# Turning the normed tiles of a second pass through DRAM and VectorE instead of TensorE

## Chip, core and metric

The kernel runs on one core of one Trainium2 chip. The time is device microseconds of the whole launch; before the change three runs took 3366.73, 3371.97 and 3379.04 us, median 3371.97. Everything is 32-bit float.

## What is computed

Two layers in a row on 8 images of 32 x 32 positions and 512 channels. The first is group norm, multi-head attention and a residual. The second samples 256 places of the image by learned offsets (a depthwise convolution, gelu, a small projection, tanh, bilinear gather), attends from all 1,024 positions to these, projects, adds the input, and ends with a layer norm and a gelu layer. The part that the change touches is the end of the second layer:

```python
z = msa + x                      # msa = att @ mo_w + mo_b
z_ln = layernorm(z, ln_g, ln_b)
out = gelu(z_ln @ mlp_w + mlp_b) + z
```

The kernel folds `ln_g` into the weights (`wm = ln_g * mlp_w`) and `ln_b` into the bias row `bm_row`, so that only `(z - mean) * rstd` has to be turned and multiplied.

## The kernel before

The first pass (layer one) runs to about 2100 us and is not touched. The second pass works by half images: `hi` from 0 to 15, each half with 512 query positions, and by head pairs `hp` from 0 to 3. One head pair of one half image is a unit, n = 4 hi + hp, 64 in all.

The order of work is written out by hand. `at(place, step)` puts a step on a list, and `run_due` sorts the list by place and calls the steps, each of which issues its instructions on all engines. Each engine then keeps this program order, since `InOrder` (L43) tells the scheduler to. So a place such as n + 0.03 sets only what stands before what on each engine; it is no time. A unit's steps in `unit_steps` (L1188) are: the scores at n; the first head's turned weights written to DRAM (`moved`, L134) at n + 0.02; the sums turned and written (`share`) at n + 0.039; the second head's turned weights at n + 0.04; both read back (`taken`, L147) and the sums spread (`spread`) up to n + 0.0411; the next unit's query projection at n + 0.042; the product with the values at n + 1.1, that is in the next unit; and its scaling to `attH` at n + 1.2.

The attention weights are thus turned already in the way that the change uses elsewhere: VectorE's `transpose` works within blocks of 32 x 32, and writing to DRAM and reading back in another order moves whole blocks between partitions.

`back_steps` (L1107) ends a half image: four tiles of 128 positions, one per unit, at n = 4 (hi + 1) + 1 + t. A tile's steps are `fetch` (the input rows `xr`, by SP's queue), `add` (on GpSimd), `joined` (output projection `wo`, sum `z` and its statistics), `norm` (`zn`, on VectorE), `turned` (four TensorE transposes of 128 x 128 into PSUM and two ScalarE copies to `zT`), `mlp` (the product with `wm`), `biased` (`res`, on VectorE), and by pairs of tiles `gelu` and `end` (the sum with `z` and the store, on GpSimd). `turned` stands at n + 0.6, behind the product of the unit before; `mlp` of a tile stands in the next unit, behind that unit's `joined`. On TensorE a unit therefore reads: scores, `wo` product, `wm` product of the tile before, queries, product with values, four transposes.

Beside this run, up to about unit 41, the last eight chunks of the depthwise convolution (`conv_steps`, L1217), in two lanes: lane 0 multiplies and adds on VectorE, five taps to a unit and three in units with n mod 8 of 3, 4 or 6; lane 1 multiplies on ScalarE into `parts` and adds on GpSimd, seven taps to a unit. And `point_steps` (L1242) prepares the sampled places of the next image b: `corners` on VectorE, `gather` (four indirect DMAs) and `sample` (four VectorE operations over 512 words) for each half of the places. With last = 8 b - 4, the samples stand at last + 0.0415 and last + 2.0415, ahead of that unit's scaling, and keys and values follow in the unit with n mod 8 = 7 and after.

`load_small` (L867) and `load_late` (L1258) load vectors and weights before unit 0. The SP queue issues DMAs in program order, and an instruction that waits there holds up those behind it.

Of the kernel before, what the change touches and what calls it, by code (L numbers as in the profile page):

```python
# [9 lines left out]
F32 = mybir.dt.float32  # L10
I32 = mybir.dt.int32
AF = mybir.ActivationFunctionType
ALU = mybir.AluOpType
# [4 lines left out]
P = 128  # L18
# [3 lines left out]
C = 512  # L22
NC = C // P
# [11 lines left out]
SQ = 32  # L35
NSQ = P // SQ
# [211 lines left out]
def attention_then_deformable_attention(  # L248
# [30 lines left out]
    nc = tc.nc  # L279
# [4 lines left out]
    dram = ctx.enter_context(tc.tile_pool(name="dram", bufs=1, space=DRAM))  # L284
# [18 lines left out]
    def load_w(pool, w, name):  # L303
        t = pool.tile([P, NC, w.shape[1]], F32, tag=name, name=name)
        nc.sync.dma_start(t, by_chunk(w))
        return t
# [100 lines left out]
    with ExitStack() as l0:  # L407
# [3 lines left out]
        nc = InOrder(tc)  # L411
# [383 lines left out]
        for b in range(B):  # L795
            first = b * per
            for hp in range(1, NHP):
                places = first_places if b == 0 else pair_places
# [19 lines left out]
            for hp in range(NHP):  # L818
                for qt in range(NT):
                    n = first + hp * NT + qt  # L820
                    if n % per == 0 and b > 0:
# [6 lines left out]
                    t = qkv[b, hp]  # L828
# [5 lines left out]
                        q=t["q", qt // NQT][:, ts(qt % NQT, P)],  # L834
# [8 lines left out]
    with ExitStack() as l1:  # L843
        nc = tc.nc
# [22 lines left out]
        def load_small():  # L867
            with nc.allow_non_contiguous_dma(reason="small vectors onto partitions"):
                for t, v in (
                    (bvk, mk_b), (bv_c, bv), (bvv, mv_b), (bqq, mq_b), (bq_c, bq), (lng, ln_g),  # L870
                    (lnb, ln_b),
                ):
                    nc.sync.dma_start(t, v.rearrange("(c p) -> p c", p=P))

        def load_conv():
            with nc.allow_non_contiguous_dma(reason="small vectors onto partitions"):
# [227 lines left out]
        def tmp(name, bufs):  # L1104
            return work.tile([P, C], F32, tag=name, name=name, bufs=bufs)

        def back_steps(hi, start, step, tail=False):  # L1107

            b, half = divmod(hi, 2)
            xs = mid[b].rearrange("(t p e) c -> e t p c", e=2, p=P)[half]  # L1110
            outs = out_tok[b].rearrange("(t p e) c -> e t p c", e=2, p=P)[half]
            xr, z, zn, zT, res = {}, {}, {}, {}, {}
            n_units = 2 * B * NHP

            def fetch(t):
                xr[t] = tmp("xr", 4)
                nc.sync.dma_start(xr[t], xs[t])

            def add(t):
                nc.gpsimd.tensor_tensor(xr[t], xr[t], bo_row, ALU.add)  # L1120

            def joined(t):
                ps = project(lambda c: attH[hi][:, c, ts(t, P)], lambda c: wo[:, c, :])
                z[t] = tmp("z", 4)
                nc.vector.tensor_tensor(z[t], ps, xr[t], ALU.add)
                stats = work.tile([P, 6], F32, tag="stats", name="stats")
                mv = xr["mv", t] = work.tile([P, 3], F32, tag="mv", name="mv")
                nc.vector.bn_stats(stats, z[t])
                nc.vector.bn_aggr(mv[:, 0:2], stats)
                rstd(mv[:, 2:3], mv[:, 1:2], 1e-5)  # L1130

            def norm(t):
                zn[t], mv = tmp("zn", 2), xr["mv", t]
                nc.vector.tensor_scalar(
                    zn[t], z[t], mv[:, 0:1], mv[:, 2:3], ALU.subtract, ALU.mult
                )

            def turned(t):
                ps = mm_tile()
                for c in range(NC):  # L1140
                    nc.tensor.transpose(ps[:, ts(c, P)], zn[t][:, ts(c, P)], ident)
                zT[t] = tmp("zT", 2)
                for half in range(2):
                    nc.scalar.copy(zT[t][:, ts(half, C // 2)], ps[:, ts(half, C // 2)])

            def mlp(t):
                res["ps", t] = project(lambda c: zT[t][:, ts(c, P)], lambda c: wm[:, c, :])

            def biased(t):
                res[t] = tmp("res", 3)  # L1150
                nc.vector.tensor_tensor(res[t], res["ps", t], bm_row, ALU.add)

            def gelu(t):
                nc.scalar.activation(res[t], res[t], AF.Gelu)

            def end(t):
                (nc.vector if tail else nc.gpsimd).tensor_tensor(res[t], res[t], z[t], ALU.add)
                (nc.sync if tail else nc.gpsimd).dma_start(outs[t], res[t])

            for t in range(NC):  # L1160
                over, eve = (start + step * t >= n_units - i and not tail for i in range(2))
                n, pair = start + step * t, start + step * (t - t % 2)

                ends = (n + 0.6, n + 1.03, n + 1.0392)
                if eve:
                    ends = (n + 0.61, n + 0.72, n + 0.73) if over else (n + 1.06, n + 1.62, n + 1.625)
                places = (pair - 1.6, pair - 0.5), (n + 0.012, n + 0.03), ends
                if tail:
                    turn = n + 0.15 + 0.005 * (t > 0)
                    places = (n - 0.7, n - 0.6), (n, n + 0.01), (turn, n + 0.25, n + 0.26)  # L1170
                steps = (fetch, add), (joined, norm), (turned, mlp, biased)
                for place, what in zip(sum(places, ()), sum(steps, ())):
                    at(place, lambda t=t, what=what: what(t))


                ends = [t - 1, t] if t % 2 and not tail else [t] if tail else []

                for what, after in (
                    (gelu, 0.27 if tail else 0.735 if over else 1.72),
                    (end, 0.28 if tail else 0.74 if over else 2.24),  # L1180
                ):
                    for i in ends:
                        at(n + after, lambda i=i, what=what: what(i))
# [33 lines left out]
        def conv_steps():  # L1217
            for lane, chunks in enumerate(((0, 3, 6), (1, 2, 4, 5, 7))):
                free = 0.5 + lane
                for k in chunks:  # L1220
                    b, cb = EARLY + k // NC, k % NC
                    first = next(n for n in range(60) if n + 0.49 > free)
                    fills = [first + 0.49, first + 0.55]
                    at(fills[0] - 1.8, lambda b=b, cb=cb: conv_fetch(b, cb))
                    for par, place in enumerate(fills):
                        at(place, lambda b=b, cb=cb, par=par: fill(b, cb, par))
                        at(place + 0.02, lambda lane=lane, par=par: fill_end(lane, par))
                    unit = int(fills[1]) + 1
                    i = 0
                    while i < KS * KS:  # L1230
                        points = unit % (2 * NHP) in (NHP - 1, NHP, NHP + 2)
                        count = 7 if lane else 3 if points else 5
                        for j in range(count):
                            if i == KS * KS:
                                break
                            place = 0.25 + 0.01 * j if not lane else 0.045 + 0.001 * j if j < 4 else 0.65 + 0.01 * j
                            at(unit + place, lambda b=b, cb=cb, i=i, lane=lane: tap(b, cb, i, lane))
                            free = unit + place
                            i += 1
                        unit += 1  # L1240

        def point_steps(b):  # L1242
            last = 2 * NHP * b - NHP
            at(last - 3.5, lambda: conv_load(b))
            at(last - 2.035, lambda: conv_gelu(b))
            at(last - 1.465, lambda: offsets(b))
            at(last - 1.36, lambda: offsets_turned(b))
            at(last - 0.959, lambda: targets(b))
            for h, (p0, p1) in enumerate(((-0.28, 0.0415), (1.72, 2.0415))):
                at(last + p0, lambda h=h: gather(b, h))  # L1250
                at(last + p1, lambda h=h: sample(b, h))
            first = 2 * NHP * b
            for hp, place in enumerate((-0.82, -0.815, 0.185, 1.18)):
                at(first + place, lambda hp=hp: key_step(b, hp))
            for t, place in enumerate((-0.81, 0.18)):
                at(first + place, lambda t=t: value_step(b, t))

        def load_late():  # L1258
            nonlocal bq_row, wo, wm, bo_row, bm_row
            bq_row = load_row(wp, bq, "bq_row")  # L1260
            wo = load_w(late2, mo_w, "wo")
            wm = load_w(late2, mlp_w, "wm")
            bo_row = load_row(late, mo_b, "bo_row")
            bm_row = load_row(late2, mlp_b, "bm_row")
            load_conv()
# [66 lines left out]
```

## Time and profile before

| | |
|---|---|
| median of three runs | 3371.97 us |
| profiled execution, whole | 3374.83 us |
| its span, first to last instruction | 3373.1 us |
| TensorE busy | 3282.7 us, 97% |
| VectorE busy | 2490.4 us, 74% |
| ScalarE busy | 1809.0 us, 54% |
| GpSimd busy | 1548.1 us, 46% |
| mean granted TensorE clock | 0.991 |

Groups of instructions that the change touches, all in the second pass, as the view by groups gives them:

| engine, operation | count | busy us | mean ns of one |
|---|---|---|---|
| PE, transposes of zn | 256 | 41.8 | 286 |
| ScalarE, copies to zT | 128 | 41.1 | 373 |
| VectorE, zn from z | 64 | 39.4 | 615 |
| VectorE, sq from e (128 x 1,024 words) | 640 | 766.1 | 1228 |
| VectorE, rsT from rs (128 x 32 words) | 128 | 27.1 | 212 |
| VectorE, taps of lane 0 | 144 | 109.4 | 760 |
| VectorE, samples (first of four, and the others) | 16 and 48 | 8.6 and 58.0 | 540 and 1209 |
| PE, wm product | 1024 | 230.7 | 592 |

Matmuls overlap in TensorE's pipeline, so the mean of one is longer than the busy time divided by the count. All instructions carry line 54, since a helper issues them; they are told apart by the tiles they write and read, written out<-in. From issue to landing a DMA took, in the median, 2.7 us (sq_d), 4.5 us (et from sq_d), 2.4 us (rs_d), 5.3 us (inv) and 6.0 us (xr).

### The profile page before, as it was taken

How to read it: one execution, taken by the hardware profiler on the slowest of the kernel's cores; microseconds unless marked ns; L12 is line 12 of the kernel's file. 1: busy time of each engine (PE TensorE's matmuls, PEld its weight loads, DVE VectorE, ACT ScalarE, POOL GpSimd, SP SyncE). 2: the span in 40 equal slices, each digit the busy share in tenths (PEclk: the TensorE clock that was granted, in tenths of full speed). 3: DMA queues.
4: the chain of work that ended last, by engine and by line, in shares of the span. 5: the costliest groups of instructions: out<-in, count | busy, mean ns of one | idle time of the engine just before them, and what ended most of it. 6: DMA issues, size and time to landing. Idle time of an engine off the chain costs nothing. (4 is left out here: it accounts for less than half of the span.)

```text
span 3373.1 us, 59630 instructions
## 1 busy us (share of the span) xinstructions
PE 3282.7 (97%) x21736; PEld 1339.8 (40%) x21736; DVE 2490.4 (74%) x3373; ACT 1809.0 (54%) x3927; POOL 1548.1 (46%) x1903
## 2 busy tenths in 40 slices
PE   7999999999999999999999998889999999999998
PEld 3344444444444344344344443433333333333333
DVE  5777788888888898888888886238667686665654
ACT  3443355576566566567567562135556555654442
POOL 1001226646746755764765663305555454642222
PEclk9999999999999999999999999999999999999999
DMA  5666766776766776766777766546666665665653
GB/s 150 179 179 164 209 181 186 223 182 183 214 188 181 210 201 181 210 197 183 204 196 184 203 193 180 170 139 220 192 206 198 191 200 187 214 218 191 224 181 127
DMA packets 446645, 642.56 MB, mean 190 GB/s; under 512 B 77105, under 2 KB 240945, under 8 KB 444305
## 3 DMA queue, kind: packets, MB, share of 16 engines
q1 hardware_dynamic: 415712, 536.67, 55.0%
q0 software_dynamic: 29488, 100.00, 9.7%
q8 instruction: 172, 2.82, 0.4%
q10 hardware_dynamic: 1152, 2.10, 0.2%
q14 instruction: 121, 0.98, 0.1%
HBM read 246.38 MB, written 123.73 MB: 110 GB/s over the span
## 5 line engine op out<-in xcount | busy, mean ns | idle before, releaser
L54 ACT ACTIVATE e<-sc,nmax 128x1024 f32<-128x1024 f32 (+1 forms) x1024 | 802.0, 796 | 494.5 <-DVE nmax L54 493.1
L54 DVE TENSOR_REDUCE nmax<-sc 128x1 f32<-128x1024 f32 (+1 forms) x640 | 751.3, 1214 | 337.5 <-PE sc L54 336.8
L54 POOL TENSOR_TENSOR oa<-part_x,oa 128x256 f32<-128x256 f32 x852 | 639.6, 751 | 554.0 <-ACT part_x L54 507.6
L54 DVE STREAM_TRANSPOSE sq<-e 128x1024 f32<-128x1024 f32 x640 | 766.1, 1228 | 155.8 <-ACT e L54 134.6
L54 ACT ACTIVATE part_x<-pad_x,dww_x 128x256 f32<-128x256 f32 x852 | 440.9, 545 | 250.3 <-POOL oa L54 249.4
L54 PE MATMUL sc<-k,q 64*64 64x512 f32 x4096 | 516.6, 602 | 13.5 <-ACT e L54 10.3
L54 PE MATMUL av<-et,v 128*64 128x256 f32 x4096 | 502.1, 388 | 15.1 <-DMA et<-sq 14.2
L54 PE MATMUL mm<-xT,wqkv 128*64 128x512 f32 x2048 | 463.5, 595 | 3.2 <-issue 3.2
L54 PEld LDWEIGHTS av<-et,v 128*64 128x64 f32 x4096 | 275.5, 137 | 332.6 <-issue 169.8
L54 POOL TENSOR_TENSOR chunk<-parts,chunk 128x256 f32<-128x256 f32 x240 | 188.8, 787 | 268.5 <-ACT parts L54 254.5
L54 POOL TENSOR_TENSOR mv<-mv,minus_half 128x1 f32<-128x1 f32 x128 | 76.3, 596 | 510.4 <-DVE mv L54 509.8
L54 PEld LDWEIGHTS sc<-k,q 64*64 64x64 f32 x4096 | 139.3, 132 | 321.8 <-issue 205.0
L54 PEld LDWEIGHTS mm<-xT,wqkv 128*64 128x64 f32 x2048 | 148.6, 138 | 255.0 <-issue 239.6
L54 DVE SCALAR_TENSOR_TENSOR od<-pad_x,dww_x,od 128x256 f32<-128x256 f32 x276 | 232.0, 841 | 5.5
L54 PE MATMUL mm<-wo,attH 128*64 128x512 f32 x1024 | 233.7, 598 | 0.0
L54 PE MATMUL mm<-wqkv,xT 128*64 128x256 f32 x2048 | 232.1, 379 | 0.0
L54 PE MATMUL mm<-wm,zT 128*64 128x512 f32 x1024 | 230.7, 592 | 1.0 <-ACT zT L54 1.0
L54 PE MATMUL mm<-w,attT 128*64 128x512 f32 x1024 | 229.8, 592 | 1.8 <-DVE attT L54 1.8
L54 PE MATMUL mm<-hat_h,wqq 128*64 128x512 f32 x1024 | 230.8, 593 | 0.0
L54 ACT ACTIVATION_READ_ACCUMULATOR e<-sc,nmax 128x1 f32 x1024 | 209.3, 204 | 0.0
L54 ACT ACTIVATE parts<-pad,dww 128x256 f32<-128x256 f32 x240 | 126.4, 551 | 126.8 <-POOL chunk L54 125.9
L54 PEld LDWEIGHTS mm<-wqkv,xT 128*64 128x64 f32 x2048 | 147.9, 137 | 77.8 <-issue 6.4
(164 smaller groups left out, 3361.8 us busy)
## 6 DMA issues: line engine op xcount, KB each, us to landing
et<-sq SPq DMA_DIRECT2D x2048, 128.0 KB, 2.8
sq_d<-sq SPq DMA_DIRECT2D x128, 512.0 KB, 2.7
et<-sq_d SPq DMA_DIRECT2D x128, 512.0 KB, 4.5
inv<-rs_d SPq DMA_DIRECT2D x256, 128.0 KB, 5.3
hat_h<-hat_d SPq DMA_DIRECT2D x16, 1024.0 KB, 8.4
xr<-mid SPq DMA_DIRECT2D x64, 256.0 KB, 6.0
x<-in_x_dram POOLq DMA_DIRECT2D x60, 256.0 KB, 4.4
out_dram<-res POOLq DMA_DIRECT2D x60, 256.0 KB, 3.6
```

The costliest lines, as they stand in the source:

```text
L54: return self.tc.keep_in_program_order(op(*args, **kwargs))
```

## The change

For 58 of the 64 tiles `turned` is replaced by three steps. `away` (n + 0.0301, right behind `norm`) writes `zn` to a DRAM tile in four DMAs, one for each 32 partitions, in runs of 128 words. `back` (n + 0.0395, behind the sums' write and ahead of the second head's turned weights) reads it in one DMA, 512 words in a row for each partition, into another buffer of the `zn` tag. `blocks` (n + 0.21, behind the scaling) turns it on VectorE in 32 x 32 blocks into `zT`. The last two tiles of the order before the end and the four of the last half image keep `turned`; there `norm` writes its columns in another order (`by_matmul`).

A turned tile now has its channels in another order over the partitions: partition 32 r + i of chunk c holds channel 128 r + 32 c + i. So `wm`, `lng` and `lnb` are loaded in that order, each in four DMAs of 32 partitions.

Other places move too. `fetch` and `add` of a pair of tiles come one unit earlier (from pair - 1.6 and pair - 0.5 to pair - 2.6 and pair - 1.45). `end` goes from 2.24 to 2.0125, ahead of the lane 1 taps of its unit. Both `sample` steps go from 0.0415 to 0.22 of their unit, behind `attH`'s scaling and behind `blocks`. Lane 0 has two taps, not three, in the units with n mod 8 of 3, 4 or 6.

```diff
-                    (bvk, mk_b), (bv_c, bv), (bvv, mv_b), (bqq, mq_b), (bq_c, bq), (lng, ln_g),
-                    (lnb, ln_b),
+                    (bvk, mk_b), (bv_c, bv), (bvv, mv_b), (bqq, mq_b), (bq_c, bq),
...
+                for t, v in ((lng, ln_g), (lnb, ln_b)):
+                    for r in range(NSQ):
+                        nc.sync.dma_start(
+                            t[ts(r, SQ)], v.rearrange("(r c i) -> r i c", r=NSQ, c=NC)[r]
+                        )
...
             def norm(t):
                 zn[t], mv = tmp("zn", 2), xr["mv", t]
+                to, src = zn[t], z[t]
+                if by_matmul(t):
+                    to = to.rearrange("p (c r i) -> p r c i", r=NSQ, c=NC)
+                    src = src.rearrange("p (r c i) -> p r c i", r=NSQ, c=NC)
                 nc.vector.tensor_scalar(
-                    zn[t], z[t], mv[:, 0:1], mv[:, 2:3], ALU.subtract, ALU.mult
+                    to, src, mv[:, 0:1], mv[:, 2:3], ALU.subtract, ALU.mult
                 )
+
+            def by_matmul(t):
+                return tail or start + step * t >= n_units - 1
+
+            def away(t):
+                zn["d", t] = dram.tile([NSQ, SQ, NSQ, P], F32, tag="zn_d", name="zn_d", bufs=3)
+                for k in range(NSQ):
+                    nc.sync.dma_start(
+                        zn["d", t][:, :, k].rearrange("r q x -> q r x"),
+                        zn[t][ts(k, SQ)].rearrange("q (r x) -> q r x", r=NSQ),
+                    )
+
+            def back(t):
+                zn["l", t] = tmp("zn", 2)
+                nc.sync.dma_start(zn["l", t], zn["d", t].rearrange("r q k x -> (r q) (k x)"))
+
+            def blocks(t):
+                zT[t] = tmp("zT", 2)
+                nc.vector.transpose(
+                    zT[t].rearrange("p (c k q) -> p k c q", c=NC, q=SQ),
+                    zn["l", t].rearrange("p (k c i) -> p k c i", k=NSQ, i=SQ),
+                )
...
-                ends = (n + 0.6, n + 1.03, n + 1.0392)
+                ends = (n + 0.0301, n + 0.0395, n + 0.21, n + 1.03, n + 1.0392)
...
-                places = (pair - 1.6, pair - 0.5), (n + 0.012, n + 0.03), ends
+                places = (pair - 2.6, pair - 1.45), (n + 0.012, n + 0.03), ends
...
-                steps = (fetch, add), (joined, norm), (turned, mlp, biased)
+                turns = (turned,) if by_matmul(t) else (away, back, blocks)
+                steps = (fetch, add), (joined, norm), (*turns, mlp, biased)
...
-                    (end, 0.28 if tail else 0.74 if over else 2.24),
+                    (end, 0.28 if tail else 0.74 if over else 2.0125),
...
-                        count = 7 if lane else 3 if points else 5
+                        count = 7 if lane else 2 if points else 5
...
-            for h, (p0, p1) in enumerate(((-0.28, 0.0415), (1.72, 2.0415))):
+            for h, (p0, p1) in enumerate(((-0.28, 0.22), (1.72, 2.22))):
...
-            wm = load_w(late2, mlp_w, "wm")
+            wm = late2.tile([P, NC, C], F32, tag="wm", name="wm")
+            for r in range(NSQ):
+                nc.sync.dma_start(
+                    wm[ts(r, SQ)], mlp_w.rearrange("(r c i) o -> r i c o", r=NSQ, c=NC)[r]
+                )
```

## Prediction

> **What bounds the kernel.** I read the table of stretches first, then the timeline of a quiet unit, then of a crowded one, then waits and DMA issues. A unit is one head pair of one half image; the second pass runs 64 (0 to 63) from 2217.7 us on. The table (stretch, length, busy time and instructions of PE, weight loads, VectorE, ScalarE, GpSimd, then granted clock, DMA share, GB/s):
>
> ```profile
> 2270.00:2345.00 75.00, 67.89 (x438) 26.02 (x432) 63.90 (x102) 43.08 (x130) 42.14 (x49) 0.95 0.74 235
> 2345.00:2930.00 585.00, 573.89 (x3528) 217.33 (x3528) 412.27 (x671) 332.51 (x912) 304.53 (x357) 1.00 0.61 197
> 2930.00:3306.00 376.00, 376.00 (x2380) 144.66 (x2376) 225.15 (x359) 181.22 (x530) 115.75 (x129) 1.00 0.63 204
> ```
>
> TensorE is full in the last stretch and almost full in the middle one (convolution taps beside attention); in the first VectorE is nearly as busy. So a TensorE instruction taken away is worth its time unless VectorE, whose order is fixed, falls behind. One quiet unit on PE (start, us, work):
>
> ```profile
> 2997.39 1.96 PE L54 MATMUL sc<-keys,q 64*64 64x256 f32 x32
> 2999.28 3.65 PE L54 MATMUL mm<-wo,attH 128*64 128x512 f32 x16
> 3002.76 3.60 PE L54 MATMUL mm<-wm,zT 128*64 128x512 f32 x16
> 3006.19 3.60 PE L54 MATMUL mm<-hat_h,wqq 128*64 128x512 f32 x16
> 3009.63 1.89 PE L54 MATMUL av<-et,vals 128*64 128x512 f32 x8
> 3011.45 0.66 PE L54 MATMUL mm<-ident,zn 128*128 128x128 f32 x4
> 3012.03 0.45 PE L54 MATMUL sc<-keys,q 64*64 64x256 f32 x4
> ```
>
> No gap; the unit is 3012.03 - 2997.39 = 14.64 us, as most are. VectorE in crowded unit 23 (start 2609.58), lines between left out:
>
> ```profile
> 2610.96 3.92 DVE L54 SCALAR_TENSOR_TENSOR smp<-row,wt,smp 128x512 f32<-128x512 f32 x3
> ...
> 2615.40 5.55 DVE L54 SCALAR_TENSOR_TENSOR chunk<-pad,dww,chunk 128x256 f32<-128x256 f32 x3
> 2620.88 2.34 DVE L54 TENSOR_REDUCE nmax<-sc 128x4 f32<-128x1024 f32 x2
> ...
> 2624.88 1.25 DVE L54 STREAM_TRANSPOSE sq<-e 128x1024 f32<-128x1024 f32 x1
> 2626.04 0.51 DVE L54 TENSOR_SCALAR zn<-z,mv 128x512 f32<-128x512 f32 x1
> ```
>
> Here samples and taps push nmax 11.3 us into the unit, where unit 40 has it at 2.0. From nmax to the end of zn is 2626.55 - 2620.88 = 5.7 us without a wait.
>
> **Gain.** Four transposes take 0.59 us from start to start. The order of after against before shows 58 of 64 tiles losing them: 58 x 0.59 = 34.2 us. The Trainium skill, "TensorE: Matmul & The Clock Gate", Part 4, gives about 275 ns for a transpose inside a kernel. The trace has 273 each, but they overlap: one after the other 58 x 1.1 = 64 us, by the row 34, which I take. Against the change speaks "VectorE: DVE Perf Modes", "Rules for kernel authors": a 128x128 transpose belongs on TensorE if PSUM will do. Obeyed, it gives 0 of 34 here; but TensorE is the full engine, VectorE is busy 60% in the last stretch (225.15/376), so the rule alone doesn't decide. ScalarE's 116 copies of 0.37 us go beside other work: nothing.
>
> **The new path.** After zn, SP issues four writes and a read that waits for all four; VectorE's blocks wait for the read.
> - Four issues: writes from 32 partitions into DRAM are not in the trace. Nearest is et<-sq, 32 partitions too, 0.61 us per issue; 128 partitions take 0.32 to 0.37. With 0.04 between, the fourth starts 3 x 0.65 = 1.95 us after the first.
> - Landing of the fourth (64 KB): rs_d, 16 KB, 2.4 us; et<-sq, 128 KB, 2.8. I take 2.4.
> - Read of 256 KB: x<-in_x_dram by SP 2.9 us, xr<-mid behind two other reads 6.0, et<-sq_d (512 KB) 4.5. It meets little in its queue: 2.9, and 0.1 for two hand-overs.
> So X = 1.95 + 2.4 + 2.9 + 0.1 = 7.4 us. Low end 3 x 0.37 + 2.0 + 2.9 + 0.1 = 6.1; high end, with sixteen et<-sq issues in 12.2 us, 3 x 0.76 + 2.9 + 4.5 + 0.1 = 9.8. "DMA: Bandwidth & Descriptors", "Anatomy of one DMA", fits 2.0 us plus bytes at 436 GB/s: 2.15 and 2.6 here, X = 6.8, and a sum 11 us better than mine; its DMAs come from GpSimd, so the rows decide.
> - Blocks: sq takes 1.23 for 1,024 words, rsT 0.21 for 32: 0.7 us for 512.
>
> **Loop and cushion.** blocks stand ahead of samples, taps and the next nmax, so VectorE has a loop: 5.7 + X + 0.7 = 13.8 us, plus 4.1 where samples come (0.54 + 3 x 1.21; they move from ahead of the scaling to behind blocks), plus 0.77 per tap. TensorE's unit is now 14.05. In a quiet unit zn ends 9.1 us in (unit 41), so blocks end 9.1 + 7.4 + 0.7 - 14.05 = 3.1 us into the next unit; the wm product needs them at 5.4. The cushion is 2.3 us. Carried from unit to unit (nmax not before scores are done; z not before 5.6; a late wm product holds all behind it; scores two units on wait for the exponentials, 5 us after nmax begins):
> - Plain units: 13.8 < 14.05, no wait, gain kept. With five taps 17.6, but these lie mostly in units of 16 to 23 us (keys, values, fills).
> - Samples without taps (units 44/46, 52/54): nmax 7.2 in, blocks 7.0 into the unit after, TensorE waits 1.6; the second sample meets a 21 us unit. 2 x 1.65 = 3.3.
> - Samples with taps (20/22, 28/30, 36/38): nmax of unit 21 at 10.4, scores wait 1.3, blocks at 8.8, wm product waits 3.4, the next again 3.4: 8.3, 7.6 and 8.3, together 24.2. In 12/14 two long units absorb it but for 1.5. In 4/6, at the start, by the same steps about 7 (estimate).
> Waits after: 36. They replace those that before has in the same places, where VectorE is late already: units 15, 21, 23, 29, 30, 31, 37, 38, 39 exceed their kind's 14.64 or 21.70 by 12.8 us, and unit 5 waits 2.0 for zn: 14.8.
>
> **Moves, together.** Taps three to two in crowded units only spread the same 49 over more units: included. xr is fetched and added a unit earlier, res added ahead of taps: this clears GpSimd where its adds held parts 7.2 us in unit 21; not counted. Five more issues per unit cost SP 2.9 us. sq_d of head 1 stands behind the waiting read, so it and et and inv behind it come 2.4 us later: et lands about 7 us into the next unit, av reads at 12.2; without that cover 2.4 us a unit. DMA gets 30 MB in 1,090 us more, 28 on 200 GB/s: hidden. In the prologue six more vector loads delay raw mv by 2 us (issued 2131.7, used 2149.2), three more wm loads delay o by 2 (it lands some 5 us before its use): hidden. Norm in 32-word runs for the last six tiles: at most 1 us.
>
> **Sum.** -34.2 + 36 - 14.8 + 1 = -12 us. The profiled run took 3374.83 us (span 3373.1, 1.7 around it): 3363. The median 3371.97 is 2.9 lower: 3360. I say 3361.
>
> **Rivals.**
> - **The turn through memory decides against it.** Place: blocks on VectorE, waiting for the read. From X = 7.65 even the plain loop exceeds 14.05; from about 7.9 the waits eat the gain. X = 8.5 makes 63 + 9 of waits: +23, 3395; X = 9.8: 3453. For it: xr's 6.0, five waits chained; GpSimd stretching VectorE's ops (three taps 5.55 us above). Against: queue empty at that moment. Chance 0.34.
> - **Cushion holds nearly everywhere.** X = 6.1 leaves 18 us of waits: -30, 3342. For it: earlier xr and ScalarE's relief; against: 0.61 issues. Chance 0.11.
> - **No change**, X about 7.6 to 8.1: 3362 to 3382. Chance 0.18.
> - Forecast, 10 to 22 us less: 0.37. Its own range 3350 to 3362.
> That the transposes stay is excluded by the order. About 0.3%, 10 us, can be told from no change: faster 0.11 + 0.37 = 0.48, same 0.18, slower 0.34. Range 3338 to 3402 (X from 6.1 to 8.6, with a few us for the estimate at the start).
>
> **What would show it.** No ident,zn but six tiles; plain units of 14.05; landing to blocks 7.4 us after zn; wm waiting for zT on VectorE only after units with samples; head 1's et landing before av needs it. Wrong if plain units exceed 14.2, or zT waits appear in quiet ones.

## The result and the profile after

| | before | after |
|---|---|---|
| median of the runs shown together | 3372.52 us (4 runs, 3366.73 to 3379.04) | 3409.51 us (4 runs, 3405.05 to 3415.02) |
| ratio, 95% interval | | 1.011, 1.0086 to 1.0134 |
| profiled execution, whole | 3374.83 us | 3415.02 us |
| its span | 3373.1 us | 3413.3 us |
| mean granted TensorE clock | 0.991 | 0.983 |

The changed kernel is slower by 37 us; 12 us less had been forecast. The three stretches of the prediction in the profile after (stretch, length, busy time and instructions of PE, weight loads, VectorE, ScalarE, GpSimd, then granted clock, DMA share, GB/s; the last one is longer here, to 3340, since the pass is):

```profile
2270.00:2345.00 75.00, 62.11 (x386) 23.74 (x384) 57.94 (x96) 38.02 (x118) 37.10 (x45) 0.93 0.76 236
2345.00:2930.00 585.00, 553.80 (x3324) 207.34 (x3321) 398.87 (x672) 307.60 (x819) 284.64 (x343) 0.98 0.69 217
2930.00:3340.00 410.00, 389.44 (x2402) 147.25 (x2400) 250.93 (x415) 176.94 (x511) 125.87 (x143) 0.98 0.73 229
```

TensorE, full in the last stretch before (376.00 of 376.00), now idles there for 20.6 us (410.00 - 389.44), and in the middle one for 31.2 where it was 11.1. The clock column fell too, from 1.00 to 0.98 in both. Both columns are needed, as the whole second pass shows in one row, first of the kernel before, then of after:

```profile
2217.70:3367.90 1150.20, 1122.60 (x6886) 425.25 (x6886) 753.09 (x1215) 589.51 (x1667) 478.09 (x552) 0.99 0.61 195
```

```profile
2222.30:3407.80 1185.50, 1111.79 (x6654) 415.79 (x6654) 764.70 (x1273) 557.17 (x1551) 467.37 (x552) 0.97 0.68 215
```

232 TensorE instructions are gone. At 0.59 us for four they should take 34.2 us of busy time with them; it fell by only 1122.60 - 1111.79 = 10.8. The rest, 23.4 us, is the same matmuls taking longer. Most of that is the clock: in this pass TensorE was busy at half clock for 16.2 us before and for 52.0 after, and half of the difference, 17.9 us, is lost. About 3.5 us more (an estimate from the two traces) are ends of matmuls, which overlap the next one's start unless a wait follows: 1.1 us at 11 waits between products before, 4.6 us at 32 after. For the last 2 us I have no place. Idle time rose from 27.6 to 73.7 us (sum of gaps over 0.1 us between TensorE's instructions; all idle times of the pass below are such sums). -34.2 + 46.1 + 23.4 = +35.3, which is what the pass grew by. Of the remaining 4.8 us of the profiled difference, 4.5 lie before its first scores, where the executions of all kernels here differ by as much (first scores between 2213.9 and 2227.0 us).

The gain itself is exact. A plain unit after, on PE (start, us, work), is 3290.21 - 3276.16 = 14.05 us, as forecast, against 14.64 before:

```profile
3276.16 1.96 PE L54 MATMUL sc<-keys,q 64*64 64x256 f32 x32
3278.04 3.65 PE L54 MATMUL mm<-wo,attH 128*64 128x512 f32 x16
3281.53 3.60 PE L54 MATMUL mm<-wm,zT 128*64 128x512 f32 x16
3284.96 3.60 PE L54 MATMUL mm<-hat_h,wqq 128*64 128x512 f32 x16
3288.39 1.89 PE L54 MATMUL av<-et,vals 128*64 128x512 f32 x8
3290.21 0.45 PE L54 MATMUL sc<-keys,q 64*64 64x256 f32 x4
```

Where the new waits are, two lines of the costliest groups say (busy us, mean ns | idle before, and what ended it):

```profile
L54 PE MATMUL mm<-wm,zT 128*64 128x512 f32 x1024 | 252.7, 639 | 49.8 <-DVE zT L54 48.7
L54 DVE STREAM_TRANSPOSE zT<-zn 128x512 f32<-128x512 f32 x58 | 41.3, 711 | 207.6 <-DMA zn<-zn_d 207.6
```

TensorE waits for zT (48.7 us), and VectorE stands 207.6 us in front of the blocks, waiting for the read. The mean of a wm matmul rose from 592 to 639 ns: the lower clock, shown below, falls on the very product that waits.

### One unit in which all of it meets

Unit 44 starts at 3025.50 and took 23.59 us, 14.64 before. Its story starts a unit earlier, with SP's queue (start, us, issues; `sq_d` are the turned weights on their way out, `et` the same read back for `av`, the product with the values, and `inv` the spread sums):

```profile
3018.86 2.15 SPq L54 DMA_DIRECT2D xr<-mid  x2
3021.05 0.94 SPq L54 DMA_DIRECT2D hat_h<-hat_d  x1
3022.34 0.32 SPq L54 DMA_DIRECT2D sq_d<-sq  x1
3022.76 3.59 SPq L54 DMA_DIRECT2D zn_d<-zn  x4
...
3032.14 0.34 SPq L54 DMA_DIRECT2D zn<-zn_d  x1
3032.57 0.38 SPq L54 DMA_DIRECT2D sq_d<-sq  x1
```

Two xr of 256 KB, hat_h of 1 MB and the first head's weights are under way when the four writes are issued. The fourth is issued at 3025.4 and lands at 3032.1, 6.7 us later, where 2.4 had been reckoned; only then is the read issued, and it takes 4.4. The write of the second head's weights, ready on VectorE at 3024.1, goes 8.4 us late behind it. VectorE meanwhile (idle time before, and what ended it, in brackets):

```profile
3029.31 0.69 DVE L54 TENSOR_TENSOR attH<-av,inv 128x512 f32<-128x512 f32 x1
3036.58 0.71 DVE L54 STREAM_TRANSPOSE zT<-zn 128x512 f32<-128x512 f32 x1 [6.58 <-DMA zn<-zn_d]
3037.22 2.32 DVE L54 TENSOR_REDUCE nmax<-sc 128x4 f32<-128x1024 f32 x2
```

and TensorE:

```profile
3025.50 1.96 PE L54 MATMUL sc<-keys,q 64*64 64x256 f32 x32
3027.39 3.65 PE L54 MATMUL mm<-wo,attH 128*64 128x512 f32 x16
3037.44 6.58 PE L54 MATMUL mm<-wm,zT 128*64 128x512 f32 x16 [6.39 <-DVE zT L54]
3043.83 3.61 PE L54 MATMUL mm<-hat_h,wqq 128*64 128x512 f32 x16
```

The wait is 6.39 us, and then the product takes 6.58 instead of 3.60. The clock column (last but two) in steps of 0.5 and 2 us shows why:

```profile
3032.50:3033.00 0.50, 0.00 (x0) 0.00 (x0) 0.00 (x0) 0.00 (x0) 0.50 (x1) 1.00 0.50 131
3033.00:3033.50 0.50, 0.00 (x0) 0.00 (x0) 0.00 (x0) 0.00 (x0) 0.21 (x1) 0.62 0.91 168
...
3039.00:3041.00 2.00, 2.00 (x8) 0.65 (x6) 1.93 (x4) 1.99 (x6) 0.00 (x0) 0.50 0.97 327
3041.00:3043.00 2.00, 2.00 (x8) 0.67 (x6) 1.49 (x4) 2.00 (x11) 1.65 (x2) 0.50 0.49 142
3043.00:3043.50 0.50, 0.50 (x4) 0.10 (x2) 0.45 (x1) 0.50 (x3) 0.20 (x2) 0.64 0.00 0
3043.50:3044.00 0.50, 0.50 (x6) 0.22 (x4) 0.41 (x2) 0.02 (x1) 0.50 (x1) 1.00 0.34 131
```

The last matmul ended at 3031.05. The clock goes to half at about 3033.1 and returns at about 3043.4, 5.9 us after the matmuls came back. Nmax of unit 44, behind the blocks, starts 11.7 us into the unit, so the next unit's weights are late as well: the lateness is handed on.

### The profile page after: what moved, and what is told of

Read it like the earlier page. It is cut to its first block, busy times and chain, and to the rows that moved or that the text cites. A ratio compares the mean times of both kernels' runs of the same rounds, so it can differ in the third digit from the quotient of the medians.

```text
span 3413.3 us, 59709 instructions
## 1 busy us (share of the span) xinstructions
PE 3274.7 (96%) x21504; PEld 1330.2 (39%) x21504; DVE 2505.4 (73%) x3431; ACT 1776.7 (52%) x3811; POOL 1537.2 (45%) x1903
## 5 line engine op out<-in xcount | busy, mean ns | idle before, releaser
L54 PE MATMUL mm<-wm,zT 128*64 128x512 f32 x1024 | 252.7, 639 | 49.8 <-DVE zT L54 48.7
L54 POOL TENSOR_TENSOR chunk<-parts,chunk 128x256 f32<-128x256 f32 x240 | 180.7, 753 | 207.8 <-ACT parts L54 193.4
L54 DVE STREAM_TRANSPOSE zT<-zn 128x512 f32<-128x512 f32 x58 | 41.3, 711 | 207.6 <-DMA zn<-zn_d 207.6
```

Source lines behind the costliest of these rows:

```text
L54: return self.tc.keep_in_program_order(op(*args, **kwargs))
```

## The experiments

Theories, as the expectations name them. **A**: the turn makes zT late because VectorE stands in front of an unlanded read with nmax queued behind; TensorE waits, and its clock falls after the wait. **B**: the other moves of the change cost it (samples, taps), or VectorE's sheer load. **C**: the traffic of the trip costs it. **D**: the waiting read holds up the second head's weights on SP's queue. All numbers stand in one table at the end of the section. Its times are medians; its waits are those of one profiled execution each, which can lie off the median (by 9.8 us in e11, 9.7 in e5, 6.5 in e13).

### e1: everything but the turn

```diff
             def by_matmul(t):
-                return tail or start + step * t >= n_units - 1
+                return True
...
-                ends = (n + 0.0301, n + 0.0395, n + 0.21, n + 1.03, n + 1.0392)
+                ends = (n + 0.6, n + 1.03, n + 1.0392)
```

> The changed kernel with all 64 tiles turned by TensorE again (identity products, ScalarE copies, at their old place); everything else of the change is kept: samples behind the scaling, two taps instead of three in crowded units, xr fetched and added a unit earlier, res stored earlier, second weights in the new row order. Theory A (the turn through memory makes zT late, TensorE waits for it, and its clock falls after the wait): the other moves are worth little, 3372 us within 12, waits of the wm product for zT near 0. Rival B (the moves cost it: samples and taps late on VectorE): the loss stays and the 34 us of gain are gone too, 3415 to 3445 us.

3375.07 us, ratio 1.0004 (0.9995 to 1.0012). Idle time 25.2 us in place of 27.6. The moves together are worth nothing either way; single units trade places (unit 13 from 21.5 to 14.6 us, unit 15 from 22.2 to 28.6, as a convolution fill moves). The whole loss, and the lost gain, belong to the turn through memory. B's first half falls: without the turn the moves cost nothing. With the turn in place they weigh again (e12, e15).

### e2, e5: the wm product later

```diff
-                ends = (n + 0.0301, n + 0.0395, n + 0.21, n + 1.03, n + 1.0392)
+                ends = (n + 0.0301, n + 0.0395, n + 0.21, n + 1.15, n + 1.215)   # e2
+                ends = (n + 0.0301, n + 0.0395, n + 0.21, n + 1.05, n + 1.215)   # e5
```

> The changed kernel with the wm product moved in the next unit from ahead of the query product to behind the attention product av, and the addition of its bias behind the next blocks: 5.5 us more of a cushion for zT. Theory A: waits of the wm product for zT fall from 49.8 us to under 8, the mean granted clock rises from 0.983 to 0.988 or more, and the time falls to 3335 to 3355 us, below before. Rival B (VectorE as a whole is too late, so that the waits only move to scores and av): 3385 to 3410 us, with scores and av waiting 25 us more than in the changed kernel.

> The changed kernel with the wm product moved behind the query product but still ahead of av (in e2_mlp_late it also went behind av and pushed av 3.6 us forward, onto et). Theory A with the lesson of e2: zT gets 3.6 us more, av keeps its place; waits for zT fall from 49.7 to 10 to 18 us, those of av stay at 8 to 14: 3360 to 3378 us. Rival B (VectorE is late as a whole, so every product of the unit becomes due too early): the waits add up to 60 us again, on zT and et: 3395 to 3415.

Both missed what A expected; e5 came out in the range of rival B, and e2 above both ranges. e2: 3422.76 us (1.0149, 1.0132 to 1.0166); the waits of wm for zT went to nothing, and av waited 49.9 us in their place, 42.0 of it for et. e5: 3404.34 us (1.0096, 1.0077 to 1.0115), its interval overlapping that of after; zT and the PSUM tile of the bias 11.0, av 18.1, scores 12.0, offsets and values 10.5. VectorE still stood before the read for 279.6 us in e2 and 234.5 in e5. A consumer that asks later doesn't help while the producer's own loop is as long as before: the wait moves to the next product that this loop feeds.

### e3: filling the wait

```diff
             def mlp(t):
+                if start + step * t in (14, 43, 53) and not tail:
+                    project(lambda c: attH[hi][:, c, ts(t, P)], lambda c: wo[:, c, :])
```

> The changed kernel with one product more (sixteen matmuls of 128x512, a repeat of the wo product into a PSUM tile that nobody reads) ahead of the wm product in the units 15, 44 and 54, where TensorE waits 5.3, 6.4 and 5.2 us for zT: 10.8 us of work added inside these waits. Theory A with the clock: the idle time is cut to 2.8 us or less, the clock stays at 1.00 there, wm in unit 44 takes 3.6 us instead of 6.6, and the three units get shorter by 2 to 3.5 us each: 3400 to 3404 us, though more is computed. Rival (the clock has nothing to do with the waiting): unit 44 stays at 23.6 and unit 54 at 22.2 us, time 3407 to 3412.

3407.02 us (1.0095, 1.0078 to 1.0111), which can't be told from after, and lies at the edge of the rival's range. The three units themselves: 15 from 36.3 to 33.6 us, 44 from 23.6 to 21.7, 54 from 22.2 to 18.5, together 8.3 us less with 10.8 us of work more. That the rival did not expect: it had unit 44 at 23.6 and unit 54 at 22.2. Unit 54 waited 0.8 us and ran at full clock. In unit 44 the expectation failed: a wait of 2.25 us was left, and wm still took 5.35 us. So the length of a wait that costs clock is lower than I had thought. The other units of the profiled pass took 4.5 us of it back (1181.8 against 1185.6 in all), with waits that differ from execution to execution (unit 46: 15.9 and 20.2 us).

The 16 profiles of this study give 166 waits of 0.25 us or more ahead of the wm product (136 of them for zT by the trace, the others mostly for a PSUM tile; those of the last half image, whose tiles TensorE turns, are left out). For each, the time from the first to the sixteenth start of the matmuls after it (3.06 us at full clock):

| wait, us | cases | of these slowed | the sixteen starts, us: median, longest |
|---|---|---|---|
| 0.25 to 1 | 59 | 1 | 3.06, 4.46 |
| 1 to 2 | 47 | 0 | 3.06, 3.06 |
| 2 to 3 | 20 | 11 | 4.58, 4.76 |
| 3 to 4 | 18 | 17 | 4.76, 5.98 |
| 4 and more | 22 | 22 | 5.51, 5.98 |

Waits under 2 us cost their length, those over 3 us up to 2.9 us more in this one product.

Why waits of 2 to 3 us fall on both sides, the clock itself shows. In the second pass of all 16 profiles its half-clock stretches start on a grid of 3.41 us, which has another offset in each execution, and last one, two or three such windows (in after 3.41 us nine times, 6.83 three times, 10.24 once). What counts is how long TensorE idles inside one window. Two windows of after ahead of unit 44's product, then two over the 2.92 us wait in unit 14 and the one behind them:

```profile
3029.70:3033.12 3.42, 1.34 (x8) 0.17 (x4) 0.30 (x1) 0.00 (x0) 2.81 (x3) 1.00 0.44 119
3033.12:3036.53 3.41, 0.00 (x0) 0.00 (x0) 0.00 (x0) 0.00 (x0) 1.03 (x2) 0.50 0.88 289
2459.68:2463.09 3.41, 2.11 (x10) 0.43 (x6) 0.00 (x0) 0.80 (x2) 3.28 (x4) 1.00 0.36 84
2463.09:2466.51 3.42, 1.80 (x10) 0.81 (x12) 2.54 (x5) 3.39 (x4) 2.73 (x3) 1.00 0.94 341
2466.51:2469.92 3.41, 3.41 (x20) 1.36 (x18) 3.39 (x4) 1.76 (x8) 1.89 (x2) 1.00 0.84 245
```

Idle for 2.08 us of its window, TensorE gets half the clock in the next; the 2.92 us wait lies across a border, 1.30 us on one side and 1.62 on the other, and costs no clock. Over all second passes, none of 5,117 full-clock windows with up to 1.94 us of idle time was followed by one at half clock, and all 124 with 2.0 us or more were (2 of the 6 between). One such window costs up to 1.7 us: 3.06 + 1.70 = 4.76, the table's most frequent length.

### e4: samples back ahead of the scaling

```diff
-            for h, (p0, p1) in enumerate(((-0.28, 0.22), (1.72, 2.22))):
+            for h, (p0, p1) in enumerate(((-0.28, 0.0415), (1.72, 2.0415))):
```

> The changed kernel with the samples back at their old place, ahead of the scaling and of the blocks, where VectorE otherwise waits for the read: 4.1 us of work beside a wait of about 7. Theory A: nmax of the units behind samples comes up to 4 us earlier; the waits for zT in the units 7, 13, 15, 21, 23, 31 and 39 shrink by more than half, those of 44 and 54 (whose read was late) stay: waits for zT 20 to 30 us in place of 49.8, time 3370 to 3385 us. Rival C (zT is late because of the DMA queue, not because of VectorE's order): less than 10 us won, 3400 to 3410.

3399.16 us (1.0079, 1.006 to 1.0099), between the two ranges expected, and its interval overlaps that of after. The waits for zT did fall to 27.7 us, as A said. But the wo product now waited 11.9 us, 7.1 of it for attH (in after 3.6, none for attH), since scaling stands behind the samples: idle time fell by 10.6 us where 22 had gone.

### e6, e7: the read behind the second weights' write

```diff
-                ends = (n + 0.0301, n + 0.0395, n + 0.21, n + 1.03, n + 1.0392)
+                ends = (n + 0.0301, n + 0.04005, n + 0.21, n + 1.03, n + 1.0392)   # e6
+                ends = (n + 0.0301, n + 0.04005, n + 0.21, n + 1.05, n + 1.215)    # e7
```

> The changed kernel with the read of the turned tile issued behind the write of the second head's weights instead of ahead of it on SP's queue. Theory D (the waiting read holds up that write and the two reads of the weights behind it, so et comes late): et of the second head lands about 2 us earlier, waits of av fall from 8.1 to under 4 us, those for zT stay within 5 us of 49.7: 3398 to 3407 us. Rival (the write would have waited for VectorE's transpose of the weights anyway, or the read is then later by as much): 3405 to 3415.

> Both edits of e5_mlp_mid and e6_back_behind_write: Theory A with D: waits for zT 10 to 18 us, of av under 6, clock 0.988 or more: 3350 to 3372 us. Rival B: 3390 to 3410.

e6: 3401.19 us (1.008, 1.0058 to 1.0102), in D's range, though its interval overlaps that of after. The write of the second weights, issued 2.7 us after VectorE had it in the median of after (0.03 before), was issued 0.7 us after. But av's waits were 7.7 us in place of 8.1. In after only 1.0 us of them, in unit 52, had been there to win; the rest lies in units 4 and 63, and does so in e6 too. e7: 3411.14 us (1.0119, 1.0089 to 1.0149), slower than even B expected, and the groups show what two good-looking edits did:

```profile
L54 PE MATMUL mm<-wm,zT 128*64 128x512 f32 x1024 | 236.1, 603 | 15.3 <-DVE res L54 13.5 <-ACT zT L54 1.0 <-DVE zT L54 0.8
...
L54 DVE STREAM_TRANSPOSE zT<-zn 128x512 f32<-128x512 f32 x58 | 41.2, 711 | 234.0 <-DMA zn<-zn_d 234.0
```

TensorE no longer waits for zT (0.8 us), but for the bias addition that frees a PSUM tile (13.5), at the scores for the queries (24.5), and at keys and values (15.1). ScalarE copies the queries behind the exponentials, which wait for nmax: 6.6 us in unit 14, the unit with one of the longest of these waits, 3.6 us. VectorE's 234.0 us before the read are not less than the 207.6 of after. This is A's loop again: what TensorE waits for is whatever VectorE hands over late.

### e10, e9: the blocks behind the next nmax

```diff
-                ends = (n + 0.0301, n + 0.0395, n + 0.21, n + 1.03, n + 1.0392)
+                ends = (n + 0.0301, n + 0.0395, n + 1.001, n + 1.03, n + 1.0392)   # e10
+                ends = (n + 0.0301, n + 0.04005, n + 1.001, n + 1.05, n + 1.215)   # e9
```

> The changed kernel with one edit: the blocks stand on VectorE behind the next unit's nmax instead of in front of it; the wm product, SP's order and all else as changed. Theory A (VectorE standing before the unlanded read holds up nmax, and that closes the loop): most of e9_blocks_next's gain comes from this edit: VectorE's wait for the read falls from 207.6 us to under 20, zT waits stay at 15 to 35 us since blocks now end only some 0.4 us before the product needs them, but short ones, under 2 us, that leave the clock alone: 3352 to 3368 us. Rival (the later wm product was needed as much): 3375 to 3395.

> As e7_both, and the blocks moved on VectorE behind the nmax of the next unit, so that VectorE never stands before an unlanded read while scores wait for their maximum. Theory A (the loop on VectorE through the read decides): the loop is open, VectorE's waits for the read fall from 207.6 us to under 40, zT waits under 8 us, the weights come earlier, waits of av under 6: 3335 to 3352 us, below before by 0.6 to 1.1%. Rival B (VectorE's sheer load in the crowded units decides, not its waiting): 3365 to 3400.

e9: 3354.8 us (0.9945, 0.9927 to 0.9964), under before, though 3 us over what A expected and with 20.0 us of waits for zT where under 8 had been. e10, the same move alone: 3444.4 us (1.021, 1.0188 to 1.0231), the worst of all and far outside both expectations. In its groups:

```profile
L54 PE MATMUL mm<-wm,zT 128*64 128x512 f32 x1024 | 262.3, 659 | 79.6 <-DVE zT L54 78.1 <-ACT zT L54 1.0 <-issue 0.6
...
L54 DVE STREAM_TRANSPOSE zT<-zn 128x512 f32<-128x512 f32 x58 | 40.6, 699 | 7.0 <-DMA zn<-zn_d 6.7
```

VectorE's wait for the read is gone (207.6 to 7.0), as expected, yet TensorE waits 79.6 us for zT. Unit 15 of e10 shows it (it starts at 2481.04):

```profile
2482.49 3.38 DVE L54 SCALAR_TENSOR_TENSOR smp<-row,wt,smp 128x512 f32<-128x512 f32 x3
2485.79 1.81 DVE L54 SCALAR_TENSOR_TENSOR chunk<-pad,dww,chunk 128x256 f32<-128x256 f32 x2
2487.53 2.34 DVE L54 TENSOR_REDUCE nmax<-sc 128x4 f32<-128x1024 f32 x2
2489.79 0.69 DVE L54 STREAM_TRANSPOSE zT<-zn 128x512 f32<-128x512 f32 x1
```

The blocks are done 9.4 us in, behind samples, taps and nmax; wm asks at 5.5. So A as I had put it, that the wait alone does it, is half of the matter: ahead of nmax the blocks hold up VectorE, behind it they come after all that crowds a unit. In e9, with wm 3.4 us later as well and the read behind the second weights' write, both ends fit: idle time 35.9 us, zT 20.0 of it. How much of the 90 us between e10 and e9 is which of the two was not run; undoing the read's place alone costs 24 us in e14.

### e11, e13: the trip made, but nobody waits for it

```diff
                 nc.vector.transpose(
                     zT[t].rearrange("p (c k q) -> p k c q", c=NC, q=SQ),
-                    zn["l", t].rearrange("p (k c i) -> p k c i", k=NSQ, i=SQ),
+                    zn[t].rearrange("p (k c i) -> p k c i", k=NSQ, i=SQ),
                 )
...
-                ends = (n + 0.0301, n + 0.0395, n + 0.21, n + 1.03, n + 1.0392)
+                ends = (n + 0.0301, n + 0.04005, n + 0.21, n + 1.03, n + 1.0392)   # e13 only
```

> The changed kernel in which the blocks take the normed tile itself instead of the one read back: all writes and reads of the trip are issued as before, but nobody waits for them. Left out by it: the exchange between blocks of 32 partitions, so each tile is turned inside its four bands only. Theory A: with the wait gone and all traffic kept, zT waits under 6 us, waits in all at or under the 27.6 us of before, clock 0.990 or more: 3330 to 3348 us. Rival C (the traffic, the twelve or so more queue entries and the late weights behind the waiting read cost it): 3380 to 3410.

> As e11_unwaited (blocks take the normed tile itself, so the exchange between bands of 32 partitions is left out), with the read issued behind the second weights' write on SP's queue. Theory D (the waiting read holds up the weights): waits of av for et fall from 25.4 to under 12 us, 3350 to 3366 us. Rival C (the 30 MB of traffic itself slows the weights): av keeps 20 us or more of waits, 3372 to 3388.

Both kernels leave out the exchange between the bands of 32 partitions. e11: 3380.75 us (1.0021, 1.0008 to 1.0033), which A didn't expect; it is at the edge of rival C's range, whose late weights and traffic e13 tells apart. No wait of wm for zT by VectorE is left, and et takes its place:

```profile
L54 PE MATMUL av<-et,vals 128*64 128x512 f32 x512 | 143.7, 615 | 25.4 <-DMA et<-sq_d 21.4 <-DVE attH L54 3.9
```

e13, where only the read's place on SP's queue differs: 3346.8 us (0.9923, 0.9894 to 0.9951), 34 us less; av waits 6.9 us, 1.8 of it for et:

```profile
L54 PE MATMUL av<-et,vals 128*64 128x512 f32 x512 | 129.2, 600 | 6.9 <-DVE attH L54 3.9 <-DMA et<-sq_d 1.8 <-DVE mv L54 1.2
```

Its pass, almost all at full clock:

```profile
2215.80:3333.10 1117.30, 1089.95 (x6654) 408.89 (x6654) 796.40 (x1273) 556.95 (x1551) 480.71 (x552) 1.00 0.72 228
```

With all the traffic of the trip (228 GB/s, 195 before) the gain is there: C falls. So does B's second half: VectorE is busy for 796.40 us of this pass, 764.70 in after, with the same 1,273 instructions, and the kernel is faster. D holds, and is large, but in the changed kernel it was hidden behind zT: TensorE was already late when et came. That is why e6 alone won little.

### e12, e14, e15: the fastest version, and two of its edits undone

```diff
# e12: e9 and the samples of e4
-                ends = (n + 0.0301, n + 0.0395, n + 0.21, n + 1.03, n + 1.0392)
+                ends = (n + 0.0301, n + 0.04005, n + 1.001, n + 1.05, n + 1.215)
-            for h, (p0, p1) in enumerate(((-0.28, 0.22), (1.72, 2.22))):
+            for h, (p0, p1) in enumerate(((-0.28, 0.0415), (1.72, 2.0415))):
# e14: e12 with n + 0.0395 for the read
# e15: e12 with "3 if points" for "2 if points"
```

> As e9_blocks_next, with the samples ahead of the scaling as in the kernel before, where VectorE waits for av anyway. If the 4.1 us of samples in front of nmax make what is left of the waits (12 us in the units 12 to 15, 20 to 23, 36 to 39), nmax comes earlier there: 3343 to 3352 us. If scaling is late instead, as in e4_sample_front, where the wo product waited 11.9 us for attH: 3358 to 3368.

> As e12_next_samples, with the read issued ahead of the second weights' write again, as in the changed kernel. Theory D: et comes 2 to 8 us later, waits of av rise from 6 to 15 to 25 us and some are long enough to lower the clock: 3352 to 3372 us. Rival (et has room enough in that version): within 4 us of 3344.

> As e12_next_samples, with three convolution taps instead of two in VectorE's crowded units, as before. If the tap count matters little, as the even exchange in e1_turned_back suggests: 3344 within 5 us. If 0.77 us more per crowded unit pushes blocks past the wm product there: 12 to 16 units of 0.8 us, 3352 to 3358.

e12: 3344.41 us (0.9906, 0.989 to 0.9923), faster than both kernels and 10 us under e9: the samples now stand where VectorE waits for av (88.4 us of such waits, 92.3 in e9), and scaling doesn't hold up wo, which waits for attH nowhere. Its pass and its two groups:

```profile
2222.90:3339.00 1116.10, 1087.89 (x6654) 408.25 (x6654) 791.11 (x1273) 556.68 (x1551) 474.32 (x552) 1.00 0.73 228
```

```profile
L54 PE MATMUL mm<-wm,zT 128*64 128x512 f32 x1024 | 231.5, 593 | 12.8 <-DVE zT L54 9.2 <-PE mm L54 2.5 <-ACT zT L54 1.0
...
L54 DVE STREAM_TRANSPOSE zT<-zn 128x512 f32<-128x512 f32 x58 | 40.6, 700 | 3.1 <-DMA zn<-zn_d 3.1
```

Busy time is 1122.60 - 1087.89 = 34.7 us under before: the gain, whole, though 3.3 us of it come from less time at half clock. e14: 3368.8 us (0.9986, 0.9977 to 0.9994), 24 us of e12's lead lost to the read's place alone; av waits 16.6 us in place of 6.2, and units 44, 46 and 54 take 17.7, 19.7 and 19.6 us. e15: 3354.47 us (0.9932, 0.9915 to 0.9948), 10 us over e12; the intervals overlap, but the profiled pass is 13.9 us longer, 9.9 of them idle time: with the loop open, a third tap is paid for. In e1 the tap count had no visible price.

### All runs

Second pass of the profiled executions: length, TensorE's idle time, its busy time (e3's has 10.8 us of added work; before and e1 have the 34.2 us of transposes).

| kernel | median us | length | idle | of it: wm for zT and PSUM, av | busy |
|---|---|---|---|---|---|
| before | 3372.5 | 1150.2 | 27.6 | 1.0, 5.4 | 1122.6 |
| after | 3409.5 | 1185.6 | 73.7 | 49.7, 8.1 | 1111.9 |
| e1 moves without the turn | 3375.1 | 1143.9 | 25.2 | 1.0, 7.0 | 1118.7 |
| e2 wm behind av | 3422.8 | 1187.7 | 67.0 | 1.0, 49.9 | 1120.7 |
| e3 three waits filled | 3407.0 | 1181.8 | 65.9 | 40.7, 8.1 | 1115.9 |
| e4 samples in front | 3399.2 | 1176.6 | 63.1 | 27.7, 10.0 | 1113.5 |
| e5 wm behind query | 3404.3 | 1173.2 | 58.4 | 11.0, 18.1 | 1114.8 |
| e6 read behind write | 3401.2 | 1177.9 | 72.2 | 49.5, 7.7 | 1105.7 |
| e7 e5 and e6 | 3411.1 | 1180.0 | 75.5 | 15.3, 8.5 | 1104.5 |
| e9 e7, blocks behind nmax | 3354.8 | 1122.8 | 35.9 | 20.0, 6.0 | 1086.9 |
| e10 blocks behind nmax alone | 3444.4 | 1221.0 | 98.3 | 79.6, 8.9 | 1122.7 |
| e11 trip unwaited | 3380.8 | 1147.5 | 41.2 | 1.0, 25.4 | 1106.3 |
| e12 e9, samples in front | 3344.4 | 1116.1 | 28.1 | 12.8, 6.2 | 1088.0 |
| e13 e11, read behind write | 3346.8 | 1117.3 | 27.3 | 1.0, 6.9 | 1090.0 |
| e14 e12, read ahead | 3368.8 | 1140.1 | 39.5 | 13.7, 16.6 | 1100.6 |
| e15 e12, three taps | 3354.5 | 1130.0 | 38.0 | 19.5, 5.9 | 1092.0 |

Most of what differs in the last column is the price of the clock. Half of the time that TensorE was busy at half clock is 8.1 us before, 26.0 in after, 35.4 in e10, 19.8 in e2 and in e3, and 3.3 to 4.8 in e9, e12 and e13. With that taken off, and e3's added work, the kernels without transposes come to 1,082 to 1,088 us, but for those in which av waited long for et: 1,101 in e2, 1,102 in e5, 1,096 in e11, 1,093 in e14. Their av products are broken off by waits; what else lengthens them isn't shown.

## Why the prediction was wrong

**Gain, 34.2 us: right.** Plain units are 14.05 us; e12's busy time is 34.7 lower, 31.4 with the clock taken off. (In the table of groups ahead of the prediction, sq and rsT are counted over both passes; 128 and 64 of them are in the second. Their means, which the sums use, hold.) The rule that a 128x128 transpose belongs on TensorE didn't decide, as the text said: VectorE did the turn in 0.71 us (0.7 forecast), and e12 is faster with it.

**The new path, X = 7.4 us: right in the middle, wrong at the ends.** The trace has 44 landings of the read: from the end of zn 6.36 to 14.50 us, median 7.65. In the median the fourth write starts 1.77 us after zn (1.95 forecast) and lands in 2.65 (2.4), and the read takes 2.94 (2.9). The prediction gave every tile one X and said of the read that it meets little in its queue. For the tile of unit 14 the fourth write took 6.0 us to land, beside the weights, a fetch of 512 KB, gathers and a store (X 10.6), for that of unit 43 6.7 us behind xr and hat_h (14.5), and for that of unit 53 the blocks started 9.8 us after zn. These three stand ahead of the longest waits for zT, in units 15, 44 and 54. That these neighbours made them late is read from the trace; no run moved them.

**Waits, 36 us: the step that failed first.** Mostly the same groups of units as forecast, but other sizes:

| units | forecast, us | measured, us |
|---|---|---|
| 4 to 7 | 7 | 12.9 |
| 12 to 15 | 1.5 | 11.1 |
| 20 to 23, 28 to 31, 36 to 39 | 24.2 | 20.5 |
| 44 to 47, 52 to 54 | 3.3 | 15.1 |
| all others (units 0 and 63 alone 9.0; 9.3 before) | 0 | 14.1 |

Where the loop was computed step by step, the sum nearly holds (20.5 for 24.2), but in part by luck: in each of three such groups it had wm wait some 3.4 us twice in a row, and wm waited 3.3, 0.6 and 2.8 us in units 21 to 23, once for 4.6 us in units 28 to 31, and 3.0, 0.7 and 3.9 us in units 37 to 39. It failed where lateness was said to be absorbed ("two long units absorb it", "the second sample meets a 21 us unit"): the lateness of nmax is handed on, and a late X falls there. Units 15, 44 and 54, behind the three late trips, have 5.3, 6.4 and 5.2 us of the waits. Idle time rose by 73.7 - 27.6 = 46.1 us; 36 - 14.8 = 21.2 had been reckoned. That is 24.9 us of the error.

**What a wait costs: the step that was missing.** A wait was charged its own length. But 23.4 us of the busy time that the transposes should have freed went to matmuls that take longer, 17.9 of it at the half clock behind the long waits, by the clock record, and some 3.5 at the waits' edges. The profile before held the warning: 0.95 in the stretch 2270 to 2345, the one where TensorE idled most (7.1 us of 75), a row that the prediction quoted and read for VectorE's load alone. The Trainium skill, "TensorE: Matmul & The Clock Gate", Part 1, says that the clock halves after an idle window of about 3.4 us and returns after as long a busy one; it should have been set against every forecast wait. The trace agrees that it halves, but a window need not be idle throughout: 2.0 us of a 3.41 us window were enough, so that 11 of 20 products were slowed already after waits of 2 to 3 us; and in unit 44 the return took 5.9 us of matmuls. The measurement decides. 24.9 + 23.4 = 48.3 us, which is the distance from the forecast's -12 to the measured +35.4 in the pass, but for the 1 us set for the tail.

**Moves.** That together they cost nothing is right for what stays when the turn is undone (e1). With a turn that works, the samples' new place costs 10 us (e9 against e12), and the third tap that was taken out would cost 10 (e15). One step was wrong in a way that the result alone didn't show: "sq_d of head 1 stands behind the waiting read ... come 2.4 us later", covered. The delay was 2.7 us in the median but 8.4 at most, and the cover that e11 lost was worth 34 us (e11 against e13). In the changed kernel later zT did the covering, not the spare time that I had named. Traffic and prologue were hidden as said: e13 carries all the traffic; from the last product of the first pass to the first scores it is 113.0 us before and 114.8 after, in the other runs 110.2 to 116.0.

**Rivals.** Slower than before was the side of the first one, and its place, blocks on VectorE waiting for the read, was right. Its price was not: it asked for an X of 8.5 in plain units, and these kept 14.05. The loss came from crowded units and single late trips, with the clock on top. That turning through memory must lose isn't shown: e12 does it and is 0.9% faster than before.

## What to carry to other kernels

When work moves off a full engine onto a path with a memory round trip, ask of every queue it touches, compute and DMA, what stands behind the wait; put the waiting instruction behind all that is ready, and its consumer late enough for that. Move both ends together: here each alone left the time or made it worse. And price a TensorE wait by its length: here one under 2 us cost itself, and one over 3 us nearly always up to 3 us more for the clock.

## What the runs showed that I had not expected

- Adding 10.8 us of useless matmuls inside three waits shortened these three units by 8.3 us together.
- The clock stayed at half for 10.2 us around a wait of 6.39 us, from 2.1 us after the last matmul to 5.9 us after the next.
- A write of 64 KB, median 3.0 us from issue to landing, took up to 8.8 us in unit 43, where a read of 1 MB had been issued just ahead of it on the same queue; I didn't try that fetch at another place.
